# Sums of the convolution's weights on three engines without their own pool, and images two to four loaded from the second chunk on

## The chip, the core and the metric

The kernel runs on one core of a Trainium2 chip. The core has four computing engines that each work through their own queue of instructions in order: TensorE (PE in the profile, its weight loads PEld), VectorE (DVE), ScalarE (ACT) and GpSimd (POOL). SyncE (SP) issues nearly all of the transfers, which run on 16 DMA engines. Engines wait for each other, and for transfers, by semaphores. The metric is the time of one execution on the device, in microseconds (us); lower is better.

## What is computed

A batch of four images x, each 128 channels of 64 x 64, passes two layers. The change is in the first. Cut to what matters:

```python
def layer0(x):                                   # x = group norm of the input
    x7 = conv2d(x, w7, b7, 3)                    # 7 x 7
    x5 = conv2d(x, w5, b5, 2)                    # 5 x 5
    x3 = conv2d(x, w3, b3, 1)                    # 3 x 3
    xn = nonlocal_block(x, ...)                  # attention of all 4096 pixels over all 4096
    return relu(x7 + x5 + x3 + xn + x)
x = x + layer0(gn(x))
t = to_tokens(x)
t = t + mamba_forward_and_backward(ln(t))        # layer 1: state-space layer, two directions
t = t + recurrence(ln(t))                        # batch norm and a sigmoid recurrence
```

The three convolutions are linear in the same x, so that their weights can be added first: the 5 x 5 weights lie in the middle of the 7 x 7 ones, the 3 x 3 weights in the middle of those, and the two plain additions of x are an identity times 2 at the centre.

## The kernel before

The whole batch stays in one tile `t` of 128 channels by 4 x 4096 pixels. `conv_attention` (L154) does the first layer. It goes through 32 chunks `n` of 512 queries, eight to an image (loop L493). A chunk has two parts. In the first (L504 to L508) TensorE makes scores `pf` (L391), ScalarE their exponentials `ex` (L393, four buffers), TensorE multiplies them with the values into `acc` (L402), and VectorE sums them into `es` (L406, L408). In the second part TensorE does a quarter of the convolution of two rows of blocks (`convolve`, L337): three groups of products `pm` (L332), each with a set of weights `wt` that is read from DRAM for it (L343, two buffers), and from sums of the image's pixels, `yx`, `yd` and `yf`, which GpSimd makes ahead (`forms`, L295, through `combine`, L293, and L313). The order of TensorE's instructions is written out by hand; the other engines' queues are ordered by a planner, which places an instruction by the time at which it expects it to be ready.

The convolution is done with fewer products than taps: pixels and weights are replaced by sums of them. The weights' sums are made once, in `weights` (L430), between the first scores of chunk 0 and the loop. It loads the three sets of weights (L437 to L439), adds them (L440, L441, L443), and then takes groups of three taps a, b, c to the halves of a + b + c and a - b + c. This is `thirds` (L446): for the columns of all seven rows (two calls, 896 elements per channel) and for rows 0 to 2 and 4 to 6 (two calls, 1152 elements). Then, for each of four forms `m`, it writes three sets to DRAM tiles `wd`: the sum of two sets (`both`, L466), one of them (L468), and the other with its sign turned (L470, L471). The fourth row goes to the tile `wc` (L457).

Where all this lies in memory: `w`, 7 rows of 9 taps, fills 63 blocks of 128 in the part of `t` that later holds image two and most of image three, and `free` is the 25 blocks after that, for the 5 x 5 weights and then for the intermediate sums `ac` and `hb`. The 3 x 3 weights `w3`, the third results of the rows (`new0`, `new4`) and two buffers `both` lie in a pool of their own, `l0_ws`, which ends with the function. The pool `l0_fm`, which holds `yx`, `yd`, `yf` and `wt`, is opened after it (L492) and gets the same memory. At its end `weights` loads images two to four (L472, L473, through `load`, L1541): 2 MB each, into the part of `t` that the weights have left. `statistics` (L226) takes an image's `bn_stats` (L230).

Of the kernel before, what the change touches and what calls it, by code (L numbers as in the profile page):

```python
# [10 lines left out]
F32 = mybir.dt.float32  # L11
AF = mybir.ActivationFunctionType
ALU = mybir.AluOpType
# [3 lines left out]
P = 128  # L17
# [131 lines left out]
def run(parts):  # L149
    for _ in parts:  # L150
        pass


def conv_attention(nc, tc, k, a, t, B, H, W, flags, load, mem, loads):  # L154
# [12 lines left out]
    T = H * W  # L167
# [11 lines left out]
    SLOT = ((0, 1, 7, 2), (4, 5, 8, 6))  # L179

    with ExitStack() as ctx:
        wp = ctx.enter_context(tc.tile_pool(name="l0_w", bufs=1))
        wc = wp.tile([P, 9, P], F32, name="wc")
# [28 lines left out]
        wd = [dram.tile([P, 9, P], F32, name=f"wd{i}") for i in range(12)]  # L212
# [60 lines left out]
        def rows(b, p):  # L273

            xp = xps[p % 2]
            first = 3 if p == 0 else 6
            n = min(RB + 6 - first, H - (p * RB + first - 3))
            if p == 0:
                nc.gpsimd.memset(xp[:, 0:3, :], 0.0)
            else:  # L280
                nc.vector.tensor_copy(xp[:, 0:6, :], xps[1 - p % 2][:, RB : RB + 6, :])
            nc.vector.tensor_scalar(
                xp[:, first : first + n, 3 : 3 + W],
                t[:, ds(b * T + (p * RB + first - 3) * W, n * W)].rearrange("p (h w) -> p h w", w=W),
                *gn[b], ALU.subtract, ALU.mult,
            )
            if first + n < RB + 6:
                nc.gpsimd.memset(xp[:, first + n :, :], 0.0)
# [6 lines left out]
        def forms(p, m):  # L295

            xp = xps[p % 2]  # L300
            yx = fm.tile([P, PR + 2, WP], F32, tag="yx", name="yx", bufs=1)
            combine(yx, lambda j: xp[:, j : j + 2 * PR + 3 : 2, :], m)
            yd = fm.tile([P, PR, WP], F32, tag="yd", name="yd", bufs=1)

            def both(rows, g):
                v = rows.rearrange("p (k g e) c -> p k g e c", g=2, e=2)[:, :, g]
                f = fm.tile([P, 4, KB, 2, PC + 2], F32, tag="yf", name="yf", bufs=4)
                for kx in range(4):
                    combine(f[:, kx], lambda j: v[:, :, :, j : j + 2 * PC + 3 : 2], kx)
                return v, f  # L310

            out = [[both(yx[:, 0:PR], 1)]]
            nc.gpsimd.tensor_tensor(yd, yx[:, 0:PR], yx[:, 2 : PR + 2], ALU.subtract)  # L313
            for g in range(2):
                out.append([both(yd, g)])
                if m in (0, 3):
                    out[-1].append(both(xp[:, 3 + m // 3 : 3 + m // 3 + 2 * PR - 1 : 2, :], g))
            return out
# [16 lines left out]
        ORDER = (1, 2, 0, 3)  # L335
# [49 lines left out]
        def scores(th, m0):  # L385

            out = []
            for m in range(2 * m0, 2 * m0 + 2):
                pf = ps_f.tile([P, 2, NC], F32, tag="f", name="pf")
                for e in range(2):  # L390
                    nc.tensor.matmul(pf[:, e, :], phi[HALF[e], m, :], th[HALF[e]], start=True, stop=True)  # L391
                ex = wk.tile([P, 2, NC], F32, tag="ex", name="ex", bufs=4)
                nc.scalar.activation(ex, pf, AF.Exp, scale=scale)  # L393
                out.append(ex)
            return out
# [33 lines left out]

        def weights():  # L430

            with tc.tile_pool(name="l0_ws", bufs=1) as ws:
                w = t[:, T : T + 63 * P].rearrange("p (y x o) -> p y x o", y=7, x=9)
                free = t[:, T + 63 * P : T + 88 * P]
                w5 = free.rearrange("p (y x o) -> p y x o", y=5, x=5)
                w3 = ws.tile([P, 3, 3, P], F32, name="w3")
                nc.sync.dma_start(w[:, :, 0:7, :], a["w7t"].rearrange("i (y x) o -> i y x o", y=7))  # L437
                nc.sync.dma_start(w5, a["w5t"].rearrange("i (y x) o -> i y x o", y=5))
                nc.sync.dma_start(w3, a["w3t"].rearrange("i (y x) o -> i y x o", y=3))  # L439
                nc.vector.tensor_tensor(w[:, 1:6, 1:6, :], w[:, 1:6, 1:6, :], w5, ALU.add)  # L440
                nc.vector.tensor_tensor(w[:, 2:5, 2:5, :], w[:, 2:5, 2:5, :], w3, ALU.add)  # L441

                nc.vector.scalar_tensor_tensor(w[:, 3, 3, :], k.ident, 2.0, w[:, 3, 3, :], ALU.mult, ALU.add)  # L443
                free = free.rearrange("p (n o) -> p n o", o=P)

                def thirds(g, new):  # L446

                    n = new.shape[1]
                    ac, hb = free[:, 0:n, :], free[:, 9 : 9 + n, :]
                    nc.vector.tensor_tensor(ac, g[0], g[2], ALU.add)  # L450
                    nc.scalar.mul(hb, g[1], 0.5)
                    nc.vector.scalar_tensor_tensor(g[1], ac, 0.5, hb, ALU.mult, ALU.add)
                    nc.vector.scalar_tensor_tensor(new, ac, 0.5, hb, ALU.mult, ALU.subtract)

                for s in SLOT:
                    thirds([w[:, :, s[i], :] for i in (0, 1, 3)], w[:, :, s[2], :])
                nc.scalar.copy(wc, w[:, 3])  # L457
                lots = []
                for y in (0, 4):
                    new = ws.tile([P, 9, P], F32, name=f"new{y}")  # L460
                    thirds([w[:, y + i] for i in range(3)], new)
                    lots.append([w[:, y], w[:, y + 1], new, w[:, y + 2]])
                for m in ORDER:
                    one, two = lots[0][m], lots[1][m]
                    both = ws.tile([P, 9, P], F32, tag="both", name="both", bufs=2)
                    nc.vector.tensor_tensor(both, one, two, ALU.add)  # L466
                    nc.sync.dma_start(wd[3 * m], both)
                    nc.sync.dma_start(wd[3 * m + 1], one)  # L468

                    nc.scalar.mul(two, two, -1.0)  # L470
                    nc.sync.dma_start(wd[3 * m + 2], two)  # L471
                for b in range(1, B):  # L472
                    load(b)  # L473

        phi = big.tile([P, NT // 2, P], F32, name="phi")
        gT = big.tile([P, NT, IC], F32, name="gT")
# [6 lines left out]
        for j in range(T // XT):  # L483
# [3 lines left out]
                th = queries(0)  # L487
            run(part)
        nxt = scores(th, 0)
        weights()  # L490
        loads()
        fm = ctx.enter_context(tc.tile_pool(name="l0_fm", bufs=2))  # L492
        for n in range(N):  # L493
            b, q = divmod(n, NQ)
            more = b + 1 < B and q == NQ - 1
            m = ORDER[q % QB]
            fs[n // QB, m] = forms(q // QB, m)
            if b + 1 < B and q == NQ - 3:
                gn[b + 1] = statistics(b + 1)
            if (q + 1) % QB == 0 and n + 1 < N:  # L500
                rows(*divmod(n // QB + 1, NQ // QB))
            acc = ps_v.tile([P, NC], F32, tag="v", name="acc")
            es = wk.tile([P, 2, NC], F32, tag="es", name="es", bufs=1)
            for i in range(NB):  # L504
                exs = nxt
                if i + 1 < NB:
                    nxt = scores(th, i + 1)
                values(i, exs, acc, es)  # L508
            nc.vector.tensor_tensor(es[:, 0, :], es[:, 0, :], es[:, 1, :], ALU.add)

            for i, _ in enumerate(convolve(n // QB, q % QB)):
                if i == 0:
                    if q % QB == 0 and n:
                        for m in range(n - QB, n):
                            finish(m, atts.pop(m))
                        cv.pop(n // QB - 1)
                    atts[n] = divide(n, acc, es)
                if more and i < T // XT:
                    part = keys(b + 1, i)
                    next(part)  # L520
                if i == 2 and n + 1 < N:
                    th = queries(n + 1)
                if i == 3 and n == NQ + 1:
                    mr = wk.tile([P, NT, 2], F32, tag="mr", name="mr", bufs=1)
                    stats = row_scales(nc, k, ps_c, "c", wk, t[:, 0:T], mr, mem)
                if i == 3 and n > NQ:
                    next(stats, None)
                if more and i < T // XT:
                    run(part)
            if n + 1 < N:  # L530
                nxt = scores(th, 0)
# [1068 lines left out]
```

## Time and profile before

Three runs gave 3254.68, 3245.34 and 3252.25 us, with the median at 3252.25. The profiled execution spans 3246.1 us. What bears on the change lies in its first 162 us:

| stage, us | what runs | length, us |
|---|---|---|
| 0 to 35.75 | image one, constants, statistics, keys and values of image one | 35.75 |
| 35.75 to 77.30 | chunk 0, attention; beside it the weights' sums on DVE and ACT | 41.55 |
| 77.30 to 97.33 | nothing on TensorE; transfers; `forms` of chunk 0 on GpSimd from 84.01 | 20.03 |
| 97.33 to 116.32 | chunk 0, convolution | 18.99 |
| 116.32 to 146.90 | chunk 1, attention | 30.58 |
| 146.90 to 162.01 | chunk 1, convolution | 15.11 |

The stages were cut where TensorE goes over from one line of the kernel to another. A later chunk shows what a stage costs that has nothing besides. A list of waits names who waited for whom and for how long; the chain of waits follows the work that ended last back to what released each step. Idle time of an engine counts only where that engine sets the pace.

### The profile page before, as it was taken

The page shows a single profiled execution, that of the slowest core. Times are in us where ns is not written, and L with a number is a line of the kernel's source. Part 1 is how long each engine was busy: PE and PEld are TensorE (multiplying, and loading weights), DVE is VectorE, ACT ScalarE, POOL GpSimd, SP SyncE. Part 2 cuts the span into 40 slices and gives each one's busy share as a digit, 9 for nine tenths or more (in the row PEclk, how much of TensorE's full clock was granted, in tenths as well). Part 3 has the DMA queues.
Part 4 walks back from the last instruction along what each step waited for, and adds up shares of the span by engine and source line. Part 5 has one row for each costly group of instructions (what it writes and reads, how often), then busy time and mean ns, then how long its engine had stood idle before and what let it go on. Part 6 is the DMA issues. An engine that isn't in the chain of part 4 may idle for free.

```text
span 3246.1 us, 43821 instructions
## 1 busy us (share of the span) xinstructions
PE 3045.7 (94%) x15991; PEld 1553.9 (48%) x15991; DVE 2138.7 (66%) x3440; ACT 1751.6 (54%) x3027; POOL 1765.9 (54%) x1478
## 2 busy tenths in 40 slices
PE   5799999999999999999997899999999999999986
PEld 1445454544454544445454354445444444454545
DVE  6665756667657566575665576777676767677667
ACT  4233334233333333332432777887788778888756
POOL 1575455745556637375564256556655564565554
PEclk9899999999999999999998999999999999999988
DMA  5301010101010101011011334333433433334332
GB/s 196 117 30 44 22 37 30 44 23 44 27 40 30 37 30 37 22 44 37 30 44 58 81 94 116 94 100 82 118 94 93 92 108 94 102 92 99 89 112 105
DMA packets 107245, 226.44 MB, mean 70 GB/s; under 512 B 25550, under 2 KB 29262, under 8 KB 105868
## 3 DMA queue, kind: packets, MB, share of 16 engines
q1 hardware_dynamic: 105804, 222.23, 24.1%
q8 instruction: 128, 2.10, 0.3%
q10 hardware_dynamic: 1216, 1.31, 0.1%
q14 instruction: 97, 0.79, 0.1%
HBM read 206.60 MB, written 16.90 MB: 69 GB/s over the span
## 4 chain that ended last, share of the span: by engine, by line
PE 78%; DVE 8%; ACT 5%; POOL 3%; DMA 3%; issue 2%; SPq 0%; ACTq 0%; POOLq 0%; DVEq 0%
PE pm L332 18%; PE acc L402 14%; PE pf L391 14%; PE pb L949 6%; PE px L961 3%; PE y L1080 3%; PE px L970 2%; PE acc L1422 2%; PE po L1151 2%; PE ptr L1023 2%; PE y L1088 2%; PE small L1058 1%; PE small L1035 1%; PE pm L1128 1%; DVE xT L981 1%
## 5 line engine op out<-in xcount | busy, mean ns | idle before, releaser
L393 ACT ACTIVATE ex<-pf 128x1024 f32<-128x1024 f32 x512 | 496.8, 1021 | 516.3 <-PE pf L391 501.2
L408 DVE TENSOR_TENSOR es<-es,ex 128x1024 f32<-128x1024 f32 x448 | 622.4, 1389 | 161.7 <-ACT ex L393 131.8
L391 PE MATMUL pf<-theta,phi 64*128 64x512 f32 x2048 | 515.5, 622 | 19.0 <-ACT ex L393 18.7
L402 PE MATMUL acc<-ex,gT 128*64 128x512 f32 x2048 | 492.0, 607 | 0.0
L332 PE MATMUL pm<-yf,wt 128*128 128x256 f32 x1536 | 386.0, 382 | 21.0 <-DMA wt<-wd 20.1
L1048 POOL TENSOR_TENSOR ct<-ct,Cst 128x512 f32<-128x512 f32 x128 | 167.9, 1312 | 410.2 <-DMA ct<-csmem 333.7
L332 PEld LDWEIGHTS pm<-yf,wt 128*128 128x128 f32 x1536 | 287.0, 190 | 117.6 <-issue 51.7
L391 PEld LDWEIGHTS pf<-theta,phi 64*128 64x128 f32 x2048 | 174.3, 187 | 337.9 <-ACT ex L393 220.0
L1014 ACT ACTIVATE lt<-lt,cs 128x128 f32<-128x128 f32 x1024 | 312.1, 390 | 0.0
L348 ACT COPY eo<-pm 128x256 f32<-128x256 f32 x96 | 35.7, 372 | 498.4 <-PE pm L332 498.4
L293 POOL TENSOR_TENSOR yf<-yd 128x272 f32<-128x272 f32 x256 | 303.3, 1211 | 1.3
L402 PEld LDWEIGHTS acc<-ex,gT 128*64 128x64 f32 x2048 | 127.9, 137 | 338.8 <-issue 330.0
L293 POOL TENSOR_TENSOR yf<-xp 128x272 f32<-128x272 f32 x128 | 141.8, 1133 | 203.2 <-PE pm L332 203.2
L949 PE MATMUL pb<-tl,wbc_fwd 128*64 128x512 f32 x512 | 238.4, 609 | 2.4 <-DVE xT L981 2.4
L949 PE MATMUL pb<-tl,wbc_bwd 128*64 128x512 f32 x512 | 239.0, 609 | 0.0
L293 POOL TENSOR_TENSOR yx<-xp 128x1260 f32<-128x1260 f32 x32 | 84.1, 2628 | 274.2 <-PE pm L332 207.2
L350 DVE TENSOR_TENSOR eo<-pm,eo 128x256 f32<-128x256 f32 x192 | 80.7, 420 | 168.9 <-ACT eo L348 166.2
L353 DVE TENSOR_TENSOR eo<-eo,pm 128x512 f32<-128x512 f32 x96 | 64.3, 670 | 192.3 <-PE pm L332 192.0
L1113 POOL TENSOR_TENSOR yT<-yT,zT 128x512 f32<-128x512 f32 x127 | 169.2, 1340 | 37.5 <-DVE yT L1100 33.5
L1047 DVE TENSOR_TENSOR lt<-lt,gm 128x1024 f32<-128x1024 f32 x128 | 177.6, 1387 | 1.9
L981 DVE SCALAR_TENSOR_TENSOR xT<-px,taps_bwd,xT 128x512 f32<-128x512 f32 x192 | 143.8, 749 | 9.2 <-ACT xT L975 4.3
L1080 PE MATMUL y<-lt,xdt 128*64 128x128 f32 x2048 | 142.8, 282 | 4.8 <-PE ptr L1023 4.6
(277 smaller groups left out, 5579.0 us busy)
## 6 DMA issues: line engine op xcount, KB each, us to landing
lt<-csmem SPq DMA_DIRECT2D x128, 512.0 KB, 5.8
wt<-wd SPq DMA_DIRECT2D x96, 576.0 KB, 3.7
ct<-csmem SPq DMA_DIRECT2D x256, 128.0 KB, 5.4
rs<-m SPq DMA_DIRECT2D x31, 512.0 KB, 3.8
t<-in_x SPq DMA_DIRECT2D x4, 2048.0 KB
rows<-after SPq DMA_DIRECT2D x32, 256.0 KB, 4.6
out<-t SPq DMA_DIRECT2D x4, 2048.0 KB, 14.3
tl<-scale SPq DMA_DIRECT2D x24, 256.0 KB, 5.7
```

The lines of the kernel that those rows point to most:

```text
L293: nc.gpsimd.tensor_tensor(out, at(x), at(y), op)
L332: nc.tensor.matmul(pm[:, e, :], wt, src, start=(i == 0), stop=(i == len(terms) - 1))
L391: nc.tensor.matmul(pf[:, e, :], phi[HALF[e], m, :], th[HALF[e]], start=True, stop=True)
L393: nc.scalar.activation(ex, pf, AF.Exp, scale=scale)
L402: nc.tensor.matmul(acc[HALF[e]], gT[:, 2 * m + e, :], ex[:, e, :], start=(m == 0), stop=(m == NT // 2 - 1))
L408: nc.vector.tensor_tensor(es, es, ex, ALU.add)
L949: nc.tensor.matmul(out, w[i]["bc"][:, tap, bass.ts(c, DS)], src, start=(tap == 0), stop=(tap == KC - 1),)
L981: nc.vector.scalar_tensor_tensor(at(n), px, taps[:, PAD - n : KC - n], at(n), ALU.mult, ALU.add)
L1014: nc.scalar.activation(v, v, AF.Relu, scale=-1.0, bias=m["b"]["cs"][:, d, m["i"], h : h + 1])
L1047: nc.vector.tensor_tensor(lt, lt, gm.unsqueeze(2).to_broadcast([P, ND, NHEAD, P]), ALU.mult)
L1080: nc.tensor.matmul(y[HALF[h], d, c, at[d]], m["dt"][:, d, 2 * c + h, :], m["lt"][:, d, 2 * c + h, :], start=(i % 2 == 0 and c == 0), stop= ...
L1113: eng.tensor_tensor(v, v, gr["z"][d][:, :, half(d, j // 2)], ALU.mult)
```

## The change

The weights' sums get along without the pool `l0_ws`. `w3` is loaded into the tile `wc`, which gets its own contents later. The scaled middle tap is written in place of the tap, so that `hb` goes, and the room in `free` (now 27 blocks) takes `ac` and the two `new`. `both` uses the two buffers of `wt`. With no pool to give its memory back, `l0_fm` can be opened ahead of `weights`, and GpSimd's `forms` of chunk 0 need not wait for it.

Of the sums, three kinds go from VectorE to GpSimd: `w3` into `w`, the first of each `thirds` (`ac`), and the four `both`. VectorE keeps the others, ScalarE the scalings, so that three engines share the work. Images two to four are no longer loaded at the end of `weights` but one each at the head of chunks 1, 2 and 3.

```diff
-            with tc.tile_pool(name="l0_ws", bufs=1) as ws:
-                free = t[:, T + 63 * P : T + 88 * P]
-                w3 = ws.tile([P, 3, 3, P], F32, name="w3")
...
-                nc.vector.tensor_tensor(w[:, 2:5, 2:5, :], w[:, 2:5, 2:5, :], w3, ALU.add)
+            free = t[:, T + 63 * P : T + 90 * P].rearrange("p (n o) -> p n o", o=P)
+            w5 = free[:, 0:25].rearrange("p (y x) o -> p y x o", y=5)
+            w3 = wc.rearrange("p (y x) o -> p y x o", y=3)
...
+            nc.gpsimd.tensor_tensor(w[:, 2:5, 2:5, :], w[:, 2:5, 2:5, :], w3, ALU.add)
...
-                    ac, hb = free[:, 0:n, :], free[:, 9 : 9 + n, :]
-                    nc.vector.tensor_tensor(ac, g[0], g[2], ALU.add)
-                    nc.scalar.mul(hb, g[1], 0.5)
-                    nc.vector.scalar_tensor_tensor(g[1], ac, 0.5, hb, ALU.mult, ALU.add)
-                    nc.vector.scalar_tensor_tensor(new, ac, 0.5, hb, ALU.mult, ALU.subtract)
+                ac = free[:, 0 : new.shape[1], :]
+                nc.gpsimd.tensor_tensor(ac, g[0], g[2], ALU.add)
+                nc.scalar.mul(g[1], g[1], 0.5)
+                nc.vector.scalar_tensor_tensor(new, ac, 0.5, g[1], ALU.mult, ALU.subtract)
+                nc.vector.scalar_tensor_tensor(g[1], ac, 0.5, g[1], ALU.mult, ALU.add)
...
-                    new = ws.tile([P, 9, P], F32, name=f"new{y}")
+                new = free[:, 9 * (i + 1) : 9 * (i + 2), :]
...
-                    both = ws.tile([P, 9, P], F32, tag="both", name="both", bufs=2)
-                    nc.vector.tensor_tensor(both, one, two, ALU.add)
+                both = fm.tile([P, 9, P], F32, tag="wt", name="both")
+                nc.gpsimd.tensor_tensor(both, one, two, ALU.add)
...
-                for b in range(1, B):
-                    load(b)
...
+        fm = ctx.enter_context(tc.tile_pool(name="l0_fm", bufs=2))
         weights()
         loads()
-        fm = ctx.enter_context(tc.tile_pool(name="l0_fm", bufs=2))
         for n in range(N):
...
+            if 0 < n < B:
+                load(n)
```

More of the change, by code (lines that the diff above doesn't have):

```diff
@@ L430, in weights @@
         def weights():
-            with tc.tile_pool(name="l0_ws", bufs=1) as ws:
-                w = t[:, T : T + 63 * P].rearrange("p (y x o) -> p y x o", y=7, x=9)
-                free = t[:, T + 63 * P : T + 88 * P]
-                w5 = free.rearrange("p (y x o) -> p y x o", y=5, x=5)
-                w3 = ws.tile([P, 3, 3, P], F32, name="w3")
[L437 to L440, printed above, removed]
-                nc.vector.tensor_tensor(w[:, 2:5, 2:5, :], w[:, 2:5, 2:5, :], w3, ALU.add)
[L443 to L448, printed above, removed]
-                    ac, hb = free[:, 0:n, :], free[:, 9 : 9 + n, :]
-                    nc.vector.tensor_tensor(ac, g[0], g[2], ALU.add)
-                    nc.scalar.mul(hb, g[1], 0.5)
-                    nc.vector.scalar_tensor_tensor(g[1], ac, 0.5, hb, ALU.mult, ALU.add)
-                    nc.vector.scalar_tensor_tensor(new, ac, 0.5, hb, ALU.mult, ALU.subtract)
[L455 to L459, printed above, removed]
-                    new = ws.tile([P, 9, P], F32, name=f"new{y}")
[L461 to L464, printed above, removed]
-                    both = ws.tile([P, 9, P], F32, tag="both", name="both", bufs=2)
[L466 to L471, printed above, removed]
-                for b in range(1, B):
-                    load(b)
@@ new lines, in weights @@
+            w = t[:, T : T + 63 * P].rearrange("p (y x o) -> p y x o", y=7, x=9)
+            free = t[:, T + 63 * P : T + 90 * P].rearrange("p (n o) -> p n o", o=P)
+            w5 = free[:, 0:25].rearrange("p (y x) o -> p y x o", y=5)
+            w3 = wc.rearrange("p (y x) o -> p y x o", y=3)
+            nc.sync.dma_start(w[:, :, 0:7, :], a["w7t"].rearrange("i (y x) o -> i y x o", y=7))
+            nc.sync.dma_start(w5, a["w5t"].rearrange("i (y x) o -> i y x o", y=5))
+            nc.sync.dma_start(w3, a["w3t"].rearrange("i (y x) o -> i y x o", y=3))
@@ new lines, in weights, with thirds @@
+            nc.vector.tensor_tensor(w[:, 1:6, 1:6, :], w[:, 1:6, 1:6, :], w5, ALU.add)
+            nc.gpsimd.tensor_tensor(w[:, 2:5, 2:5, :], w[:, 2:5, 2:5, :], w3, ALU.add)
+            nc.vector.scalar_tensor_tensor(w[:, 3, 3, :], k.ident, 2.0, w[:, 3, 3, :], ALU.mult, ALU.add)
+            def thirds(g, new):
+                ac = free[:, 0 : new.shape[1], :]
[3 more added lines that the diff above has]
+                nc.vector.scalar_tensor_tensor(g[1], ac, 0.5, g[1], ALU.mult, ALU.add)
@@ new lines, in weights @@
+            for s in SLOT:
+                thirds([w[:, :, s[i], :] for i in (0, 1, 3)], w[:, :, s[2], :])
+            nc.scalar.copy(wc, w[:, 3])
+            lots = []
+            for i, y in enumerate((0, 4)):
+                new = free[:, 9 * (i + 1) : 9 * (i + 2), :]
+                thirds([w[:, y + i] for i in range(3)], new)
+                lots.append([w[:, y], w[:, y + 1], new, w[:, y + 2]])
+            for m in ORDER:
+                one, two = lots[0][m], lots[1][m]
+                both = fm.tile([P, 9, P], F32, tag="wt", name="both")
+                nc.gpsimd.tensor_tensor(both, one, two, ALU.add)
+                nc.sync.dma_start(wd[3 * m], both)
+                nc.sync.dma_start(wd[3 * m + 1], one)
+                nc.scalar.mul(two, two, -1.0)
+                nc.sync.dma_start(wd[3 * m + 2], two)
```

## The prediction

> **What bounds the kernel now.** I read the page's busy line first, then the waits of the first 117 us, since the diff touches only what happens before the second query chunk.
>
> ```profile
> PE 3045.7 (94%) x15991; PEld 1553.9 (48%) x15991; DVE 2138.7 (66%) x3440; ACT 1751.6 (54%) x3027; POOL 1765.9 (54%) x1478
> ```
>
> TensorE (PE) is busy for 94% and its instructions come in one order written by hand, so an idle stretch of PE anywhere moves the end by its own length. The order of PE's instructions is the same in both builds, and on the other engines nothing of weight moves after the second chunk. So the change is worth the PE idle time that it removes before about 120 us.
>
> ```profile
> POOL yx L293 <- DMA wd<-both: 67.0, 1, 67.0
> ...
> PE pm L332 <- DMA wt<-wd: 20.1, 1, 20.1
> ...
> DVE st L230 <- DMA t<-in_x: 11.3, 1, 11.3
> ```
>
> (Columns: who waited, for whom; total us, times, longest.) The first line is the memory of the pool `l0_ws`: `l0_fm` takes its place, so the first sums for the convolution (`yx`) wait until the last `both` has left for DRAM. The second is PE waiting for the first weights of the convolution. The table of stages gives the size:
>
> ```profile
> 35.75:77.30 41.55, 33.81 (x128) 9.80 (x128) 37.03 (x34) 23.21 (x26) 0.00 (x0) 0.92 0.44 157
> 77.30:97.33 20.03, 0.00 (x0) 0.03 (x1) 8.01 (x14) 1.96 (x2) 12.15 (x14) 0.63 1.00 402
> 97.33:116.32 18.99, 18.04 (x64) 13.57 (x65) 16.88 (x27) 1.80 (x4) 6.10 (x6) 0.86 0.20 65
> 116.32:146.90 30.58, 30.25 (x129) 9.39 (x129) 21.82 (x17) 15.51 (x16) 15.52 (x10) 1.00 0.06 20
> 146.90:162.01 15.11, 15.11 (x66) 12.00 (x64) 8.64 (x13) 1.80 (x4) 8.68 (x8) 1.00 0.24 78
> ```
>
> (Stage; us, then busy us of PE, PEld, DVE, ACT, POOL; PE clock, DMA share, GB/s.) Rows 1 and 3 are chunk 0, its attention and its convolution part; rows 4 and 5 are the same work for chunk 1. Chunk 0 costs 41.55 + 20.03 + 18.99 = 80.57 us against 45.69, so **34.9 us** is all that could be had. In row 2 PE does nothing while the DMA engines are full (1.00, 402 GB/s). The chain says with what:
>
> ```profile
> 67.28 10.90 DMA wd<-both
> 78.20 1.37 DVE both L466
> 79.59 1.17 ACT t L470
> 80.78 4.38 DMA wd<-t
> ...
> 85.76 0.38 SPq L343
> 86.19 11.11 DMA wt<-wd
> 97.33 3.75 PE pm L332 x8
> ```
>
> (Start, us, what.) A 576 KB write and a 576 KB load take 10.9 and 11.1 us, because the 2 MB loads of images two to four lie in the same queue; the median of such a load on the page is 3.7.
>
> **What the Trainium skill says.** "SBUF — State Buffer", Who interferes with whom: a VectorE (DVE) instruction with two SBUF inputs and a GpSimd (POOL) instruction that reads SBUF exclude one another for a whole instruction. The trace agrees (start, us, engine, line):
>
> ```profile
> 91.47 4.84 POOL L293 TENSOR_TENSOR yf<-yd 128x272 f32<-128x272 f32 x8
> ```
> ```profile
> 120.27 11.73 POOL L293 TENSOR_TENSOR yf<-yd 128x272 f32<-128x272 f32 x8
> 121.50 6.23 DVE L408 TENSOR_TENSOR es<-es,ex 128x1024 f32<-128x1024 f32 x4
> ```
>
> The same eight sums take 4.84 us beside `bn_stats` (one input) and 11.73 beside the `es` sums (two), which themselves go from 1.22 to 1.56 us. "GPSIMD Engine Reference", Elementwise — side-by-side cycle accounting, has an fp32 sum of 2048 elements at 4497 ns on GpSimd against 2293. The trace agrees in kind: 1120 elements take 2.61 us on POOL (below), 1152 on DVE 1.35.
>
> ```profile
> L313 POOL TENSOR_TENSOR yd<-yx x2: 2602/2610/2618, 116.5 to 162.4; 128x1120 f32<-128x1120 f32 x2
> ```
>
> **The change part by part.**
>
> *Pool gone.* `yx`, `yd`, `yf` of chunk 0 have memory of their own and need only the padded rows, written at 19.63 (L282). They cost 2.37 + 2.45 + 2.54 + 4.84 = 12.2 us on POOL, and are done between 31.9 (nothing in the way) and about 36.5 (the `xn` scalings and the 3.5 us sum L440 block it). I take 35.5. The first conflict falls on `xn` for the second key block, which PE wants only at 25.4, so keys lose nothing.
>
> *Sums on POOL.* POOL is in order, so the weights' first POOL sum (`w3`) starts after these forms, at 35.5 where DVE had done it at 40.0; `w3` itself landed at 14.5 + 15.3 = 29.8. From here one chain runs through three engines, since `ac` is one buffer and every `thirds` waits for the one before:
> - a POOL sum of 1152 elements is 2.61 x 1152/1120 = 2.7 us, of 896 is 2.1. DVE's `scalar_tensor_tensor` stays at 1.08 and 1.35 (L452).
> - `w3` 2.7; two column groups: POOL 2.1, DVE 1.08 + one `es` 1.22 + 1.08, with 0.3 for the identity and one more `es`: 12.5 together; two row groups: POOL 2.7, DVE 1.35 + 1.35, with one `es` in the second: 12.0; four `both` of 2.7: 10.8. Sum 38.0.
> - the last sign flip on ACT 1.16, the three exponentials queued behind it 2.9, the last values on PE 0.9: 5.0.
> - the third `both` has the buffer of the first and waits for its write (2.9 to 4.3 us without images beside it), the fourth likewise: about 1. Hand-overs, 0.05 to 0.1 us each: about 1.5.
> - the exclusion: eight `es` sums stand where a POOL sum is ready, 1.15 us each, 9.2 in all if each bites, 0 if none. I take 6.
>
> 35.5 + 38.0 + 5.0 + 2.5 + 6 = **87.0** for the end of chunk 0's attention, against 77.3. So this stage gets longer by 9.7 us: the exponentials stand in ACT's queue behind sign flips that wait for POOL, and PE waits for them.
>
> *Weights' buffers.* The first `wt` takes the buffer of the third `both`, and stands in SP's queue behind the last sign-flipped write, issued when the flip ends, 3.8 us before that, at 83.2; with 3.7 us it lands at 86.9. So convolution starts at about 87, set by both alike, not at 97.33: **-10.3 us**. With the bounds (31.9 and no exclusion: 77.4; 36.5 and all of it: 91.2): -20 to -6.
>
> *The convolution of chunk 0.* It took 18.99 us against 15.11. Of the 3.88, some 2.7 are matmuls at half clock after 20 us without work (3.75 for eight against 1.97 later, 1.92 for `den` against 1.04) and 0.95 a wait at 105.5 for DVE. With PE little used from 60 to 83 us I expect half of that back: **-2** (0 to -3.7).
>
> *Images later.* Image two is issued after the second `wt`, at about 86, and takes the 8.1 us of image one (issued 0.81, landed 8.93): 96 with that `wt` ahead of it, while its `bn_stats` stand in DVE's queue behind the second group's sums, 12 us into the convolution, at 99. Nothing. Image three follows the third `wt` and lands near 106, where chunk 1 starts. Image four is issued when chunk 0's last weights are released, near 104, and lands by 114. Its statistics stand between the `es` sums of chunk 1, in front of the sum that falls due about 10 us into that chunk: DVE waits 1 to 3 us, four `ex` buffers take most of it up. DVE there also gets 11 `bn_stats` of 0.61 us: 21.8 + 6.7 = 28.5 of 30.6 us. **+1** (0 to +4). In before they ran in the idle stretch. The three weights' loads keep their places.
>
> Sum: -10.3 - 2 + 1 = -11.3; 3252.25 - 11.3 = **3241 us**.
>
> **The rivals.**
> - *The port rarely matters.* Forms done at 32, no exclusion: convolution at 77 to 81, its clock warm, images free: -17 - 3.5 = -20: 3232. For it: DVE often waits for POOL in this chain and has no `es` then. Against: 11.73 for 4.84.
> - *A new wait in the old place.* All eight exclusions and the late forms: 91, convolution no shorter, DVE late by 3 in chunk 1: -6 - 1 + 3 = -4: 3248. For it: every `es` that falls behind is one more that meets a `both`.
> - *Slower.* Writes and loads as slow as now: third `both` at 71.5 + 10.9, the fourth done at 88.8, its flip at 90, the first `wt` 11.3 us later at 101.3: +4; convolution -2; image four late by 5: +7: 3259. For it: the 10.9 and 11.3 of this trace. Against: the 4 MB that made them are no longer ahead.
>
> **How the numbers follow.** The forecast has 0.48, the first rival 0.28, the second 0.16, the slower one 0.08. A quarter of the forecast's own spread (some 3 us, from the exclusion) lies within 0.3% (9.8 us): faster 0.48 x 0.75 + 0.28 = 0.64, same 0.48 x 0.25 + 0.16 = 0.28, slower 0.08. The range 3230 to 3250 leaves out the slower case and the ends of the two others, some 2 in 10.
>
> **What would show it.** In the changed profile: POOL's `yx` near 20 us and no wait on `wd<-both`; POOL sums of 2.6 to 3.9 us with `es` sums between; long waits of ACT's sign flips on POOL, and of PE on ACT's `ex` between 60 and 87; the first convolution matmul near 87 and chunk 1 near 104; no wait of DVE on an image before it. The prediction is wrong if convolution starts before 80 or after 92, if chunk 1 takes more than 34 us, or if later stages change.

## The result, and the profile after

The changed kernel takes 3232.18 us, the median of 4 runs (3230.48 to 3234.81), beside 3251.31 us for the kernel before, also of 4 (3245.34 to 3254.68). The ratio is 0.9944 with a 95% interval of 0.9927 to 0.9961: 0.6% faster. The busy line of the page shows that no work on TensorE was saved (15991 matmuls in both kernels), so the gain is time in which PE stood or ran slowly:

```profile
PE 3043.7 (94%) x15991; PEld 1554.8 (48%) x15991; DVE 2140.1 (66%) x3431; ACT 1751.5 (54%) x3027; POOL 1796.9 (56%) x1487
```

The table of stages of the changed kernel has the columns of the one shown for before. Row 1 is chunk 0's attention, row 2 its convolution, rows 3 and 4 the same for chunk 1.

```profile
35.77:86.75 50.98, 34.99 (x128) 10.71 (x129) 35.12 (x26) 25.28 (x27) 29.71 (x12) 0.80 0.42 161
86.75:101.85 15.10, 15.10 (x67) 11.98 (x65) 12.69 (x20) 1.80 (x4) 6.11 (x6) 1.00 0.89 342
101.85:132.40 30.55, 30.28 (x130) 9.41 (x129) 29.79 (x36) 15.62 (x16) 11.73 (x10) 1.00 0.25 100
132.40:147.48 15.08, 15.08 (x66) 11.97 (x64) 9.80 (x14) 1.80 (x4) 8.68 (x8) 1.00 0.23 78
```

The row without any PE work, 20.03 us in before, has no counterpart: convolution follows attention without a gap. But the attention itself grew from 41.55 to 50.98 us, with POOL busy for 29.71 of them. Chunk 1 starts at 101.85 where it started at 116.32, **14.47 us** earlier, and it keeps its length (45.63 us after 45.69). DVE, which now takes the images' statistics there, is busy for 29.79 of 30.55 us, and PE loses nothing by it.

The waits of the changed kernel between 15 and 110 us (who, for whom: total us, times, longest):

```profile
PE pf L391 <- ACT ex L393: 16.3, 4, 8.5
...
ACT t L467 <- POOL both L463: 11.6, 3, 8.3
...
DVE t L449 <- POOL t L447: 7.0, 3, 2.5
...
POOL yx L293 <- DVE bsum L218: 2.7, 1, 2.7
```

The wait of `yx` for `wd<-both` (67.0 us before), the one of PE for `wt<-wd` (20.1) and the one for an image (11.3) are no longer in the list. In their place stands a row of engines: PE waits for exponentials, they stand in ACT's queue behind a sign flip, and the flip waits for POOL.

### The profile page after: what moved, and what is told of

The parts are those of the page before. It is cut to its first block, busy times and chain, and to the rows that moved or that the text cites. A ratio compares the mean times of both kernels' runs of the same rounds, so it can differ in the third digit from the quotient of the medians.

```text
span 3233.0 us, 43827 instructions
## 1 busy us (share of the span) xinstructions
PE 3043.7 (94%) x15991; PEld 1554.8 (48%) x15991; DVE 2140.1 (66%) x3431; ACT 1751.5 (54%) x3027; POOL 1796.9 (56%) x1487
## 4 chain that ended last, share of the span: by engine, by line
PE 78%; DVE 6%; POOL 5%; ACT 5%; DMA 3%; issue 2%; SPq 0%; POOLq 0%; ACTq 0%; DVEq 0%
PE pm L332 18%; PE acc L402 14%; PE pf L391 14%; PE pb L946 6%; PE px L958 3%; PE y L1077 3%; PE px L967 2%; PE acc L1419 2%; PE po L1148 2%; PE y L1085 2%; PE ptr L1020 2%; PE small L1055 2%; PE small L1032 1%; PE pm L1125 1%; DMA ct<-csmem 1%
## 5 line engine op out<-in xcount | busy, mean ns | idle before, releaser
L1110 POOL TENSOR_TENSOR yT<-yT,zT 128x512 f32<-128x512 f32 x127 | 168.2, 1333 | 37.9 <-DVE yT L1097 32.7
```

Source lines behind the costliest of these rows:

```text
L1110: eng.tensor_tensor(v, v, gr["z"][d][:, :, half(d, j // 2)], ALU.mult)
```

## The experiments

Two theories of the gain. **A**: it comes from what no longer stands behind something else, that is the forms of chunk 0 behind the pool's memory and the first weights behind 6 MB of images; the move of the sums to GpSimd brings nothing. **B**: it comes from VectorE, which three engines' work relieves. The first five runs take the three parts of the change alone and in pairs: pool gone (with all that it brought to the memory, so also `w3` in `wc`, the taps scaled in place and `both` in the buffers of `wt`), loads later, sums on GpSimd. In each diff the lines are those of the kernel named.

**Loads later, alone** (from before):

```diff
-                for b in range(1, B):
-                    load(b)
...
+            if 0 < n < B:
+                load(n)
```

> The kernel before with one part of the change alone: images two to four are loaded at the heads of chunks 1 to 3; the pool of the weights' sums and the sums on VectorE stay. Theory A (the gain is that neither the forms on GpSimd nor the first weights from DRAM stand behind something else any more; the sums on GpSimd bring nothing): the forms still wait for the pool until 84 us, but the weights no longer lie behind 4 MB of images, so that the convolution of chunk 0 waits for the first forms only and starts at 88 to 91 instead of 97.3; chunk 1 starts at 105 to 109 instead of 116.3, total 3241 to 3246. Theory B (the gain is the work taken from VectorE): VectorE has all its sums, so chunk 1 starts at 113 to 117 and the total is 3248 to 3254.

Measured: 3240.89 us, ratio 0.9966 (0.9954 to 0.9979). Convolution starts at 89.35, chunk 1 at 107.85, 8.47 us earlier than in before. The waits of this run:

```profile
POOL yx L293 <- DMA wd<-both: 68.4, 1, 68.4
...
PE pm L332 <- DMA wt<-wd: 13.8, 2, 12.5
```

The forms still wait for the pool, and the first weights are issued only when the last write has left (85.24), but with no image right ahead of them the first product starts 4.1 us after their issue, and not 11.6 (85.76 to 97.33 in before). That is most of the difference. The first `yf` is ready at 88.41, only 0.9 us ahead of that product, so the forms were nearly as late as the weights. One image is still issued early, at 66.12 (64.44 in before), and the write of the second `both` behind it takes 10.6 us, so that the edit takes two of the three images out of the way, and not all.

**Pool gone, alone** (from the changed kernel, so that the two other parts are undone):

```diff
-            nc.gpsimd.tensor_tensor(w[:, 2:5, 2:5, :], w[:, 2:5, 2:5, :], w3, ALU.add)
+            nc.vector.tensor_tensor(w[:, 2:5, 2:5, :], w[:, 2:5, 2:5, :], w3, ALU.add)
...
-                nc.gpsimd.tensor_tensor(ac, g[0], g[2], ALU.add)
+                nc.vector.tensor_tensor(ac, g[0], g[2], ALU.add)
...
-                nc.gpsimd.tensor_tensor(both, one, two, ALU.add)
+                nc.vector.tensor_tensor(both, one, two, ALU.add)
...
+            for b in range(1, B):
+                load(b)
...
-            if 0 < n < B:
-                load(n)
```

> The changed kernel with its sums back on VectorE and the images loaded at the end of the weights again, so that only the pool is gone. Theory A: the forms are made by 37 us, but the first weights stand behind three images (6 MB at the 402 GB/s of before are 15 us): convolution at 97 to 103, chunk 1 at 112 to 119, total 3247 to 3256; so the pool alone brings nothing. Theory B: likewise no gain, 3248 to 3254.

Measured: 3247.49 us, ratio 0.9991 (0.9982 to 1.0000). Chunk 1 starts at 119.60, 3.28 us later than in before, although the median is 3.0 us below that of before (3250.51; more on this below the table). PE stands for the weights even longer:

```profile
PE pm L332 <- DMA wt<-wd: 26.5, 1, 26.5
```

So the forms are ready (at 37.3), and it doesn't help: what ended last was not the forms but the weights behind the images.

**Pool gone and loads later, sums on VectorE** (the changed kernel with the three `nc.gpsimd` of the sums turned to `nc.vector`):

> The changed kernel with the three kinds of sums back on VectorE; the pool is gone and the images are loaded late. Theory A: convolution of chunk 0 starts at 80 to 86 instead of 86.8, since 1152 elements take 1.35 us and not 2.6 to 3.9; chunk 1 at 95 to 101, total 3226 to 3232, as good as the changed kernel or up to 6 us better. Theory B: the gain is lost or halved: chunk 1 at 108 or later, total 3241 or more.

Measured: 3234.64 us, ratio 0.9955 (0.9938 to 0.9971); chunk 1 at 102.30, against 101.85 in the changed kernel. This is nearly the whole gain without a single sum of the weights on GpSimd, though A had expected 1 to 7 us more (chunk 1 at 95 to 101). Its table of stages (attention, wait, convolution of chunk 0) shows why VectorE could be relieved for nothing:

```profile
35.75:73.64 37.89, 32.18 (x128) 9.38 (x128) 34.61 (x32) 23.32 (x26) 1.42 (x3) 0.95 0.30 112
73.64:83.88 10.24, 0.00 (x0) 0.03 (x1) 3.80 (x4) 1.93 (x2) 0.00 (x0) 0.73 1.00 377
83.88:102.30 18.42, 17.63 (x64) 13.43 (x65) 13.69 (x21) 1.80 (x4) 6.11 (x6) 0.87 0.90 364
```

With the sums on VectorE chunk 0's attention ends 13.1 us sooner (73.64 against 86.75), and PE then stands for 10.24 us with the DMA engines full, until the first weights come back from DRAM. Of these, 4.9 us pass before the load is issued, behind the writes of the later forms in SP's queue, and 5.3 after:

```profile
78.17 0.32 SPq L468 DMA_DIRECT2D wd<-t  x1
78.58 1.86 SPq L343 DMA_DIRECT2D wt<-wd  x2
```

After this idle time PE's clock is low (0.87), and the convolution takes 18.42 us where the changed kernel takes 15.10 (0.8 of the 3.3 is a second wait, for the third weights). 13.1 us gained, 10.2 and 3.3 lost: 0.4 us are left, the wrong way. The slow sums of the changed kernel fill a wait that would be there anyway, and keep PE warm through it.

**Pool gone, sums on GpSimd, loads early** (the changed kernel with the loads put back at the end of `weights`):

> The changed kernel with images two to four loaded at the end of the weights, as before. Theory A: the first weights stand behind three images again: convolution of chunk 0 at 98 to 105, chunk 1 at 113 to 120, total 3245 to 3252: the gain is gone. Theory B: VectorE is still relieved, so at least half of the gain stays: total 3240 or less.

Measured: 3250.62 us, ratio 1.0002 (0.9994 to 1.0011); chunk 1 at 119.08. Its queue of DMA issues (start, us that SP spent on it) shows the three images ahead of the weights; the first PE wait for those is 14.95 us:

```profile
81.13 4.64 SPq L1539 DMA_DIRECT2D t<-in_x  x3
85.81 29.30 SPq L343 DMA_DIRECT2D wt<-wd  x4
```
```profile
PE pm L332 <- DMA wt<-wd: 14.9, 1, 14.9
```

**Sums on GpSimd, alone** (before with the three `nc.vector` turned to `nc.gpsimd`):

> The kernel before with only the three kinds of sums moved to GpSimd; the pool and the early loads of the images stay. Theory A (it is the waits, not VectorE's work): the chain of sums starts some 5 us earlier on GpSimd than in the changed kernel, since no forms stand ahead of it, but the forms still wait for the pool and the first weights for 4 to 6 MB of images: convolution of chunk 0 at 96 to 103, chunk 1 at 112 to 119, total 3245 to 3254. Theory B (VectorE's relief brings part of the gain): chunk 1 at 111 or earlier, total 3244 or less.

Measured: 3252.02 us, ratio 1.0000 (0.9991 to 1.0009); chunk 1 at 116.40, against 116.32.

Together, the start of chunk 1 against before:

| pool gone | loads later | sums on GpSimd | chunk 1 starts, us | against before | ratio |
|---|---|---|---|---|---|
| | | | 116.32 | | 1 |
| | | x | 116.40 | +0.08 | 1.0000 |
| | x | | 107.85 | -8.47 | 0.9966 |
| x | | | 119.60 | +3.28 | 0.9991 |
| x | | x | 119.08 | +2.76 | 1.0002 |
| x | x | | 102.30 | -14.02 | 0.9955 |
| x | x | x | 101.85 | -14.47 | 0.9944 |

B falls: the sums bring +0.08, -0.52 and -0.45 us in the three pairs that differ in them alone, and by the medians +1.4, +3.1 and -2.5, of either sign. (The fourth pair, with the loads later and the pool kept, was not run.) A holds, with one refinement: the two other parts are not a sum. Pool gone brings nothing alone (+3.3 us) and -5.6 once the images are out of the way, since two things had to come before the convolution, and only removing both lets it start. In the -5.6 is also that the third image goes late only when the pool is gone: no image is issued before 80.49 then.

Differences of less than 2 us in this table say little. Each start is read from one execution, and in five of the twelve profiles, among them "loads later alone" and "pool gone alone", chunk 0 begins at 37.4 to 37.9 us and not at 35.6 to 35.9, because the second block of image one's keys took nearly twice as long (before, then loads later alone):

```profile
25.43 1.08 PE L257 MATMUL pp<-xn,pw 128*64 128x512 f32 x4
```
```profile
25.86 1.98 PE L257 MATMUL pp<-xn,pw 128*64 128x512 f32 x4
```

This occurs with and without the pool, and ahead of the weights' sums, so the edits are hardly its cause, but no run shows that. If the late start is passed on in full (an estimate from these starts), loads later alone is worth some 1.7 us more than the table says, and pool gone is +1.4 alone, not +3.3, and -3.9, not -5.6, with the images out of the way. The ends of the executions are less sharp still: what follows the last product of the convolution, whose code no edit touches, takes 1493.1 to 1503.6 us in the twelve profiles, and the least with pool gone alone. Why that kernel's median is 3 us below that of before, no run shows.

The table also leaves out what the later images cost in chunk 1. It takes 45.63 us in the changed kernel, but 46.46 with the sums on VectorE and 47.20 with loads later alone, where PE waits for exponentials, and these for VectorE, which has the images' statistics in front of its `es`. At the start of chunk 2 the changed kernel is 1.3 us ahead of the one with sums on VectorE, not 0.45.

**Later sets.** The next run asks whether the four `both` with their flips, which the prediction put on the chain, set the end of chunk 0's attention, and whether it pays to make each form's sets near the chunk that reads them. From the changed kernel:

```diff
-            for m in ORDER:
-                one, two = lots[0][m], lots[1][m]
...
+        def sets(m):
+            one, two = lots[0][m], lots[1][m]
+            both = fm.tile([P, 9, P], F32, tag="wt", name="both")
+            nc.gpsimd.tensor_tensor(both, one, two, ALU.add)
...
-        weights()
+        lots = weights()
+        sets(ORDER[0])
...
-            if 0 < n < B:
-                load(n)
+            if n < QB - 1:
+                sets(ORDER[n + 1])
+            if 2 < n < B + 2:
+                load(n - 2)
```

> The changed kernel, but each of the four forms' sets (both, the copy, the sign flip) is made when its chunk is near, not all four ahead of chunk 0, and the images are loaded from chunk 3 on. If the end of chunk 0's attention is set by the exponentials that stand behind four sums on GpSimd and four sign flips on ScalarE, as the chain of the changed kernel says, two flips fewer and two sums of 3.2 us fewer let it end at 83 to 85 instead of 86.8: chunk 1 at 98 to 101 instead of 101.9, total 3228 to 3232. If it is the first weights' way over DRAM instead, the shorter queue of writes gives at least as much: 81 to 83. If neither counts, it stays at 86 to 88.

Measured: 3243.64 us, ratio 0.9978 (0.9971 to 0.9985). Convolution starts at 87.43, no sooner than in the changed kernel (86.75), although two `both` and two flips fewer come before it: so those two were not on the chain. (Chunk 0 begins late here too, but the first `both` stands at 66.54, against 66.37.) The forecast of 83 to 85 failed, and with it that of the total. The profile is that of the slowest of 17 runs, 6.6 us above the median. Chunk 2 still starts 13.8 us ahead of before, chunk 3 only 2.8. The chain of waits in between:

```profile
144.07 2.60 POOL both L466
...
146.68 2.79 DMA wd<-both
...
149.91 10.91 DMA t<-in_x
...
160.85 0.04 DVE st L230
```

A write to DRAM waits for a `both` on POOL, and stands in SP's queue ahead of the weights and the images; the images then land so late that the `bn_stats` of two of them follow one another in VectorE's queue, between the `es` sums (the chain goes on with them until 186 us). This is the kind of wait that the prediction priced at 1 us for image four. There it didn't come; here the stretch costs 11 us. This is read from the chain: no run has the late sets without the later loads.

**No trip to DRAM.** If the wait in the kernel with sums on VectorE is the trip of the sets, taking the first four chunks' weights straight from SBUF, where they lie, must give most of those 10 us. From the kernel of later sets:

```diff
+            held[m] = both, one, two
...
-                wt = fm.tile([P, 9, P], F32, tag="wt", name="wt")
-                nc.sync.dma_start(wt, wd[3 * m + n])
+                if p == 0:
+                    wt = held[m][n]
+                else:
+                    wt = fm.tile([P, 9, P], F32, tag="wt", name="wt")
+                    nc.sync.dma_start(wt, wd[3 * m + n])
...
-            if 2 < n < B + 2:
-                load(n - 2)
+            if QB - 1 < n < QB + B - 1:
+                load(n - QB + 1)
```

It ran twice: with `w3`, `ac` and the first `both` on VectorE, and with all sums on GpSimd.

> As the late sets, and the sums are on VectorE again (GpSimd has only the late both), and chunks 0 to 3 take their weights from where they were made, not over DRAM; the images are loaded from chunk 4 on. With the sums on VectorE attention of chunk 0 ended at 73.6, and convolution waited 10.2 us for weights from DRAM. Without that way: convolution at 70 to 75, chunk 1 at 85 to 91, total 3216 to 3223. If the wait was not for the way over DRAM but for the sets themselves, convolution stays at 80 to 84 and the total at 3228 to 3234.

> As g1, with all sums on GpSimd as in the changed kernel. There attention ended after the weights had landed, so the way over DRAM was not what convolution waited for: no better than f1, chunk 1 at 98 to 101, total 3228 to 3232. If GpSimd's sums cost nothing it comes to g1's 3216 to 3223.

Measured: on VectorE 3226.59 us, ratio 0.9927 (0.9911 to 0.9944), convolution from 76.08 and chunk 1 from 91.18; on GpSimd 3233.33 us, ratio 0.9943 (0.9927 to 0.9960), from 87.51 and 102.62. The attention rows of chunk 0, first with the sums on VectorE, then on GpSimd:

```profile
35.75:76.08 40.33, 32.29 (x129) 9.52 (x129) 35.93 (x31) 23.11 (x26) 5.10 (x4) 0.96 0.31 118
```
```profile
35.75:87.51 51.76, 36.43 (x136) 11.36 (x134) 31.00 (x26) 24.59 (x28) 22.93 (x10) 0.84 0.24 92
```

With the sums on VectorE convolution starts 7.8 us sooner than with the trip (83.88), though a little later than the 70 to 75 expected, and without a gap behind the attention. The edit removes both halves of the wait, the trip and the writes of the later forms ahead of it; no run separates them. With all sums on GpSimd convolution starts where it started with the trip (87.43), as expected, since there the weights came in time; chunk 1 comes 1.6 us after the 98 to 101 forecast.

With the trip gone, the place of the sums matters after all: 11.4 us for the same sums. In the changed kernel that loss lies beside the trip and costs nothing, which is why both readings of "the move of the sums" are true, each in its own kernel.

**What is left in chunk 0.** In the first of these two a `both` of the second form stands on POOL at 63.77, beside a sum of two rows on VectorE that takes 3.79 us. The next run made the sets at the head of the chunk that reads them (`if 0 < n < QB: sets(ORDER[n])`).

> As the kernel with direct weights and sums on VectorE (chunk 0's convolution from 76.08, chunk 1 from 91.18, 3226.6 us), but the three sets of the second form, which no chunk before chunk 1 reads, are made at the head of chunk 1 and not beside chunk 0's attention. Chunk 0 loses nothing of its own work. Theory (what ends chunk 0's attention is the row of sums and sign flips in front of its last exponentials): the GpSimd sum of the second form no longer stands beside the last two-input sum on VectorE, which took 3.79 us there against 1.35 alone, and one sign flip fewer (1.1 us) stands ahead of the exponentials, so the convolution of chunk 0 starts at 72 to 74 and chunk 1 at 87 to 89; chunk 1 loses 0 to 1 us for the sets that it now makes itself; 3222 to 3226 us in all. Rival (the sums of the first form and TensorE's own pairs set the end, the second form lies beside them): start at 75.5 to 76.5, chunk 1 at 91, 3226 to 3228.

Measured: 3231.81 us, ratio 0.9949 (0.9933 to 0.9966), convolution from 76.58 and chunk 1 from 94.64. The edit didn't move the sum that it was to move. The planner places a sum when its operands are ready, so the `both` of the second form stood at 63.62 again; and the later ones now came ahead of a chunk's forms in POOL's queue, so that PE waited for `yf` (1.73 us in chunk 0, 2.20 in chunk 1). It tells nothing for or against its theory. The last run put that one sum on VectorE instead (`m in ORDER[:2]` for `m == ORDER[0]`).

> As the kernel with direct weights and sums on VectorE (convolution from 76.08, chunk 1 from 91.18, 3226.6 us), but the sum `both` of the second form is made on VectorE as well (1.35 us) and no longer on GpSimd (3.54 us). In the run just made this GpSimd sum stood at 63.6 us again, since the planner places it when its operands are ready, and the `scalar_tensor_tensor` beside it took 3.79 us again. Theory (the two exclude one another and that lies on the chain that ends chunk 0's attention): the `scalar_tensor_tensor` falls to 1.36 us, a `both` of 1.35 comes into VectorE's queue, so the convolution of chunk 0 starts 1 to 2.4 us earlier, at 73.7 to 75.1, and chunk 1 at 89 to 90; 3224 to 3226 us. Rival (3.79 us is that instruction's own wait for something else, as for the `t` columns that ScalarE scales): it stays near 3.8, and the start moves to 76 to 77.5.

Measured: 3223.32 us, ratio 0.9918 (0.9902 to 0.9935), convolution from 75.42 and chunk 1 from 90.61. The same sum on VectorE, first beside POOL's `both`, then without it:

```profile
64.74 3.79 DVE L453 SCALAR_TENSOR_TENSOR t<-t 128x1152 f32<-128x1152 f32 x1
```
```profile
66.31 1.35 DVE L453 SCALAR_TENSOR_TENSOR t<-t 128x1152 f32<-128x1152 f32 x1
```

So the 3.79 us is the exclusion of the two engines. Of the 2.4 us only 0.66 reached the start of the convolution, between the ranges of theory and rival. But this profile is one of the five in which chunk 0 begins late: its first scores stand at 37.46, not 35.90, and all sums 1.56 us later (the first at 41.75, not 40.19). Counted from the first scores, convolution comes 37.96 us after them and not 40.18, so that 2.2 of the 2.4 us arrive and the sum was on the chain. This is the fastest version measured, 27 us below before; its interval overlaps that of the kernel that it came from.

## Why the prediction was right, and where not

The forecast was 3241 us, in a range of 3230 to 3250; measured were 3232.18, inside it but near its end, with a gain larger than forecast.

- **What bounds the kernel** held: PE's busy time is the same to 2 us, and the gain lies ahead of 102 us. By the tables of stages 12.8 of the 14.5 us are idle time of PE, and 1.7 are the same matmuls done faster, a term that the prediction has too, under the convolution.
- **Forms** were done at 37.1, not 35.5, just past the later bound of 36.5. The start was right; POOL's list shows which terms were too small:

```profile
19.72 2.93 POOL L293 TENSOR_TENSOR yx<-xp 128x1260 f32<-128x1260 f32 x1 [2.72 <-DVE bsum L218]
22.73 3.81 POOL L293 TENSOR_TENSOR yf<-yx 128x272 f32<-128x272 f32 x4
26.50 2.62 POOL L313 TENSOR_TENSOR yd<-yx 128x1120 f32<-128x1120 f32 x1
29.20 7.98 POOL L293 TENSOR_TENSOR yf<-yd 128x272 f32<-128x272 f32 x8
...
52.55 3.55 POOL L447 TENSOR_TENSOR t<-t 128x1152 f32<-128x1152 f32 x1 [3.41 <-DVE A L727]
...
66.37 9.65 POOL L463 TENSOR_TENSOR both<-t 128x1152 f32<-128x1152 f32 x3 [3.87 <-DVE t L450]
```

  The last eight `yf` took 7.98 us, beside VectorE's 5 x 5 sum, where 4.84 was the price of them alone, and the first four 3.81, where 2.45 was.
- **The sums up to the first `both`** took 29.2 us (37.13 to 66.37); the steps priced them at 27.2 and added some 7.5 for hand-overs and exclusion. Exclusion is there: the four `ac` take 12.9 us where 9.6 was priced. But VectorE mostly waits for POOL in this stretch (7.0 us in the list of waits), so there is less of it than the 6 us that I took, and the identity and one `es` that I put on the chain lie beside POOL.
- **The step that failed** is the end of the chain: "four `both` of 2.7: 10.8", the last flip 1.16, "the three exponentials queued behind it 2.9", the last values 0.9, and about 1 for buffers, 16.8 in all. The chain of the changed kernel (start, us, what):

```profile
66.37 7.08 POOL both L463 x2
...
74.55 1.01 ACT ex L393
...
75.61 3.79 PE pf L391 x8
79.39 1.91 PE acc L402 x8
81.30 1.92 PE pf L391 x8
83.22 3.58 PE acc L402 x16
86.80 1.93 PE pm L332 x8
```

  Only the first two `both` are on it. After the second flip six exponentials are still to do, three of them ahead of the last flip, and PE works through their scores and values at its own pace, 11.1 us from 75.61 to 86.75, the first eight matmuls cold (3.79 against 1.92 for the next eight scores). The third and fourth `both` and their flips lie beside that; the run with later sets shows it. The end of the chain took 20.4 us, 3.6 more than priced; the sums before took 5.5 less, the forms 1.6 more. So 86.75 against a forecast of **87.0** is in part luck: errors of opposite sign that cancel.
- **The first weights** were to land at 86.9 and set the start together with the attention. They were issued at 81.22, not 83.2, and PE didn't wait for them: the attention set the start alone. That images ahead made the 11 us of before was right. The Trainium skill, "DMA: Bandwidth & Descriptors", Queues, rings and completion order, has each DMA engine consume a ring's entries in order; the runs agree, with 4.1 us from issue to the first product without an image right ahead and 14.95 of waiting with three.
- **The convolution of chunk 0** gained 3.89 us, not 2: 2.94 are faster matmuls, and 0.95 a wait of before at 105.5, which the prediction put down to DVE and for which the profile names no releaser. I expected PE half cold; it had just worked for 11 us. "TensorE: Matmul & The Clock Gate", What's actually happening, gives half the clock as the state after an idle window of about 3.4 us, and the full one after as much work. The first eight products agree: 1.97 us here, 3.75 in before and in the five runs in which PE had stood still for longer than 10 us before them.
- **Images later** cost 0, not +1. The image of chunk 1 was issued at 83.81 and the others at 93.14 and 102.32, close to the steps' times, and DVE waited for none, though 17 `bn_stats` start in chunk 1's attention and not 11. The two kernels with loads later and the sums on VectorE do lose 0.8 and 1.5 us in chunk 1.

The sum was -11.3 us; in the profiles it is -10.58 - 3.89 - 0.06 = -14.5 to the end of chunk 1. The medians differ by 19.1 us, with an interval of 12.7 to 23.7 (0.39 to 0.73% of 3251), which holds 14.5. The two profiles end 13.1 us apart: a stall of 1.6 at chunk 21, which only this profile of before has, also against runs without any gain, adds to the 14.5, and what follows the convolution's last product takes 3.0 us more in the changed kernel (1499.8 against 1496.8). What the rest of the 19.1 is, beyond the spread of the runs, no run settles. The first rival's 3232 us is what was measured, but by luck and not by its mechanism: it had the convolution start at 77 to 81.

## What to carry to other kernels

When several things must be there before a stage, taking one of them away can be worth nothing until the last one goes too (pool gone brought nothing alone, and -5.6 us with the images out of the way): list what is ready when, and price the parts of a change together. A slower engine is free as long as its work fits into a wait that stays; ask what that wait is (here the way of the sets through DRAM, with the writes queued ahead), because the better change may be to remove it. In a chain at the end of a stage, count what is left for the bounding engine after the last release: it can be longer than the queue in front of it.

## What the runs showed that I had not expected

- I had left `scalar_tensor_tensor` at its own price beside GpSimd. It is excluded like a plain sum: 1152 elements take 3.79 us beside a POOL sum and 1.35 without, and even one of 128 elements, 0.29 us without, takes 2.17 in the changed kernel, where a POOL sum of 2.95 us starts at 39.83:

```profile
40.76 2.17 DVE L442 SCALAR_TENSOR_TENSOR t<-ident,t 128x128 f32<-128x128 f32 x1
```

- A wait on PE costs twice: the 10.24 us in the kernel with sums on VectorE brought some 2.5 us of slower matmuls behind it (3.3 us more in the convolution, less the second wait of 0.8).
- Statistics that are not urgent can hold up an engine's queue when their data come late: in the run with later sets PE waited 6.3 us at one go for the last `es` of chunk 2, in a stretch that cost 11.
